# Graph layer, batch norm and attention on one core: a new order for the opening of layer 1 and for the last finished rows

## The chip, the cores and the metric

The kernel runs on one core of a Trainium2 chip. The metric is the device time of one execution in microseconds (us), lower is better; the profile's own clock runs from the first to the last instruction of the core ("the span"). A core has five engines with a queue each, worked off in program order: TensorE (PE, matrix products; its weight loads are PEld), VectorE (DVE), ScalarE (ACT), GpSimd (POOL), and SyncE (SP), which here issues all transfers. Engines wait for each other through semaphores.

## The reference, cut to what matters

Sixteen batches b of 1024 rows with 256 columns pass through two residual layers, each closed by a layer norm over the 256 columns:

```python
# layer 0: graph convolution, two linear maps with batch norm over all batches
x = layernorm(x + bn(relu(bn((A_hat @ x) @ W1.T)) @ W2.T))
# layer 1
c = mean(x, axis=-1)                                   # one number a row
Wg = adj * 2*abs(abs(sigmoid(c[None,:] - c[:,None]) - 0.5) - 0.5)
q  = relu((x.T @ Wg) * para)                           # queries, 4 heads of 64
k, v = split(x @ kv_w)
x = layernorm(x + softmax(q k.T * scale) v)
```

Everything is float32. Because the batch norms of layer 0 average over all batches, layer 1 can't start before the last batch of layer 0 is done.

## The kernel before

Layer 0 ends at about 810 us of the span. It leaves its result transposed in device memory (`yT`). From then on, `fast()` does layer 1 with a queue order that is written out by hand.

**Rows of a batch.** The 1024 rows of a batch are handled as four blocks j of 256 rows. A block goes through: `load` (fetch the transposed y and the residual x; two buffers of each, `LDP = 2`), `bn2_q` (scale and shift on POOL, line L610; for batch 0 `bn2` on ACT, L592), `rows` (DVE transpose L614 and residual add L615; for batch 0 a PE transpose `py`, L626, and an add, L628), `ln1_a` (DVE statistics L558/L559, then POOL makes the scale and shift, L66, L68, L632), `ln1_b` (ACT applies them, L642, and sums each row). For batches 0 and 1, `x1_t` transposes the finished rows on PE (`px`, L671) and DVE copies them to `x1T` (L672). Once the four blocks are there, `means` (DVE, L675 and L677) makes the row means and `crow` lays them along a row by way of a PE transpose `pc` (L688, L692).

**Work that follows the rows.** `gate` / `gate0` makes one of eight 128-row strips of Wg: `wg_a` on ACT (L706, or L708 and L709), `wg_b` on DVE (L715, L716), which takes a strip of adj from a ring of four (`AR = 4`) and asks for the next one. `keys` (`pk`, L732) and `values` (`pv`, L743) are PE products with x1T. `graph` (`pg`, L757; for batch 0 `graph0`, L1076) is the product of the rows and Wg, in eight parts for batch 0, and `queries` (DVE, L765 and L766) makes `qT` from it.

**Attention** runs in 256 steps, 16 a batch. A step has `scores` (PE, L783, into the two PSUM buffers `s`), `exps` (ACT, L795), `sums` (DVE, L801 and L804, the softmax denominators `acc`) and `attend` (PE, L819, into `o`). Four steps make up one half of the rows (hf) with one pair of heads.

**Finished rows.** After each half of a batch: `dens` (PE adds up acc over the partitions, `pd`, L846; ACT copies `dt`, L848), `recips` (PE `pr`, L857; DVE L859), `fetch_o` (the attention output comes back from device memory in another layout, `ob`; in the very last half `back` does this on PE, `pf`, L870), `finish_a` (DVE: transpose L890, product L894, residual L899, statistics; POOL: scale and shift, L66, L68, L903) and `finish_b` (ACT applies them, L911, and the block is stored).

**The order.** `put(w, t, f, ...)` hands piece f to half-turn t of batch w; a batch has NC = 8 half-turns of two steps. The main loop goes in passes of NK = 4 steps (two half-turns): `arrange` sorts all pieces of both half-turns, they are issued first, then the four steps `scores(k+1)`, `exps(k+1)`, `sums(k)`, `attend(k)`. So pieces of a half-turn with odd t are also issued at the start of the pass. The pieces of batch 0 are written out ahead of the loop; `opening(s)` issues gates and `graph0` parts in negative half-turns; and the rows of batch 1 are put there as well, through `put(b - 2, ...)` with b = 1, the four `x1_t` all in the last half-turn before the first attention step.

Of the kernel before, what the change touches and what calls it, by code (L numbers as in the profile page):

```python
# [22 lines left out]
def gnn_norm_attention_kernel(  # L23
# [17 lines left out]
    B, N, C = x.shape  # L41
    H = W1.shape[0]
    NT = N // P
# [3 lines left out]
    NH = N // FB  # L47
# [77 lines left out]
    with ExitStack() as l0:  # L125
# [32 lines left out]
        with ExitStack() as ph1:  # L158
# [9 lines left out]
            for i in range(0, NT, 2):  # L168
                t = hp.tile([P, 2, N], F32, tag="h", name=f"A{i}")
# [29 lines left out]
            for h in range(NH):  # L199
                rows = range(h * KB, (h + 1) * KB)  # L200
# [228 lines left out]
        def load(b, j):  # L429
            shape = [P, CT, 2 * P] if b == 0 else [P, 2, C]  # L430
            yts[b, j] = ldp.tile(shape, F32, tag="yt", name=f"yt{b}_{j}")
            xrs[b, j] = ldp.tile([P, 2, C], F32, tag="xr", name=f"xr{b}_{j}")
            fetch_rows(b, j)
# [16 lines left out]
        with ExitStack() as ph2:  # L450
# [74 lines left out]
            for k, pair in enumerate(pairs):  # L525
# [4 lines left out]
                if not ahead:  # L530
                    for j in range(LDP):
                        load(0, j)
                    for j in range(LDP, NT // 2):
                        t = accp.tile([P, 2, FB], F32, tag="acc", name=f"first{j}")
# [32 lines left out]
    def fast():  # L567
      with ExitStack() as fx:
# [48 lines left out]
        def begin(b):  # L617
            x1Ts[b] = x1Tp.tile([P, CT, N], F32, tag="x1T", name=f"x1T_{b}")
            css[b] = sm.tile([P, NT], F32, tag="cs", bufs=2, name=f"cs_{b}")
# [17 lines left out]
        def ln1_b(b, j):  # L637
            nm, rs = mvs.pop((b, j))
            for a in range(2):
                r = x1s[b, j][:, a, :]  # L640
                i = 2 * j + a
                nc.scalar.activation(  # L642
                    r, r, AF.Identity, bias=nm[:, a : a + 1], scale=rs[:, a : a + 1], accum_out=css[b][:, i : i + 1]
                )
# [22 lines left out]
        def x1_t(b, j):  # L667
            p = ps_t.tile([P, CT, 2 * P], F32, tag="t", name="px")
            for a in range(2):
                for c in range(CT):  # L670
                    nc.tensor.transpose(p[:, c, ts(a, P)], x1s[b, j][:, a, ts(c, P)], ident)  # L671
            nc.vector.tensor_copy(x1Ts[b][:, :, ts(j, 2 * P)], p)  # L672

        def means(b):
            nc.vector.tensor_scalar_mul(css[b], css[b], 1.0 / C)  # L675
            hcs[b] = sm.tile([P, NT], F32, tag="hcs", bufs=2, name=f"hcs_{b}")
            nc.vector.tensor_scalar_mul(hcs[b], css[b], 0.5)  # L677
# [49 lines left out]
        def keys(b, c, h):  # L727
            if h == 0:
                kTs[b, c] = kp.tile([P, N], F32, tag="kT", name=f"kT_{b}_{c}")
            p = ps_t.tile([P, FB], F32, tag="t", name="pk")  # L730
            for k in range(CT):
                nc.tensor.matmul(  # L732
                    p, kvw[:, k, ts(c, P)], x1Ts[b][:, k, ts(h, FB)], start=(k == 0), stop=(k == CT - 1)
                )
            (nc.vector.tensor_copy if b == 0 else nc.scalar.copy)(kTs[b, c][:, ts(h, FB)], p)

        def values(b, j):
            if j == 0:
                vs[b] = vp.tile([P, NT, C], F32, tag="v", name=f"v_{b}")
            p = ps_t.tile([P, FB], F32, tag="t", name="pv")  # L740
            for a in range(2):
                for k in range(CT):
                    nc.tensor.matmul(  # L743
                        p[:, ts(a, C)],
                        x1Ts[b][:, k, ts(j + a, P)],
                        kvw[:, k, C:],
                        start=(k == 0),
                        stop=(k == CT - 1),
                    )
            nc.scalar.copy(vs[b][:, j : j + 2, :], p.rearrange("p (a c) -> p a c", a=2))  # L750
# [57 lines left out]
        def by_pe(b, hf):  # L808
            return b == B - 1 and hf == NH - 1
# [134 lines left out]

        NS = NT // 2 * NP * NH
        NC = NS // 2
        at = {}

        def put(w, t, f, *a):
            at.setdefault(w * NC + t, []).append((f, a))  # L950
# [4 lines left out]
        for b in range(B):  # L955

            for hf in range(NH):
                t = (hf + 1) * (NC // NH)
                put(b, t, dens, b, hf)
                put(b, t, recips, b, hf)  # L960
                for k in range(KB // 2):
                    j = hf * (KB // 2) + k

                    t_a, t_b = (t + 2 + k, t + 6 + k) if hf == 0 else (t + 4 + k, t + 6 + k)
                    if b == B - 1:
                        t_a, t_b = (t + 2 + k, NC + 1) if hf == 0 else (t + 1 + k, t + 2 + k)
                    put(b, t if by_pe(b, hf) else t + 1, back if by_pe(b, hf) else fetch_o, b, j)
                    put(b, t_a, finish_a, b, j)
                    put(b, t_b, finish_b, b, j)
            if b == 0:  # L970
                continue

            put(b - 2, 2, begin, b)
            for j in range(NT // 2):
                put(b - 2, j, load, b, j)
                put(b - 2, j + 1, bn2_q, b, j)
                put(b - 2, j + 2, rows, b, j)
                put(b - 2, j + 2, ln1_a, b, j)
                put(b - 2, j + 3, ln1_b, b, j)
                if b == 1:  # L980
                    put(b - 2, NC - 1, x1_t, b, j)
                    continue
                put(b - 2, j + 3, put_x1, b, j)
                put(b - 2, 5 + j // 2 * 2, get_x1, b, j)
                put(b - 2, min(6 + j, NC), x1_v, b, j)
            put(b - 2, NC - 2, means, b)
            put(b - 2, NC - 1, crow, b)

            i = 0
            for t, n in enumerate(WG):  # L990
                for i in range(i, i + n):
                    put(b - 1, t, gate, b, i)
                i += 1
            kv = [(keys, (b, c, h)) for h in range(NH) for c in range(CT)]
            kv += [(values, (b, j)) for j in range(0, NT, 2)]
            for t, n in enumerate(KV):
                for _ in range(n):
                    f, a = kv.pop(0)
                    put(b - 1, t, f, *a)
            m = 0  # L1000
            for t, n in enumerate(QG):
                for m in range(m, m + n):
                    put(b - 1, NC - len(QG) + t, graph, b, m)
                m += 1
# [66 lines left out]
        def graph0(k):  # L1071
            if k == 0:
                PG0.extend(ps_s.tile([P, 2, FB], F32, tag="s", name=f"pg0_{h}") for h in range(NH))
            for h in range(NH):
                for c in range(CT):
                    nc.tensor.matmul(  # L1076
                        PG0[h][:, c, :],
                        x1s[0, k // 2][:, k % 2, ts(c, P)],
                        wgs[0, k][:, ts(h, FB)],
                        start=(k == 0),  # L1080
                        stop=(k == NT - 1),
                    )
            if k == NT - 1:
                for h in range(NH):
                    for c in range(CT):
                        queries(0, c, h, PG0[h][:, c, :])

        begin(0)
        constants_q()
        for j in range(NT // 2):  # L1090
            bn2(0, j)
        for j in range(NT // 2):
            ln1_a(0, j)
        for j in range(NT // 2):
            ln1_b(0, j)
        x1_t(0, 0)
        x1_t(0, 1)
        keys(0, 0, 0)
        x1_t(0, 2)
        x1_t(0, 3)  # L1100
        means(0)
        crow(0)
        gate0(0)
        keys(0, 1, 0)
        for c in range(CT):
            keys(0, c, 1)
        gate0(1)
        values(0, 0)
        values(0, 2)
        gate0(2)  # L1110
        values(0, 4)
        values(0, 6)

        def opening(s):

            k = s + NC
            if 0 <= k < NC:
                for i in range(3 + 2 * k, min(5 + 2 * k, NT)):
                    gate0(i)
                graph0(k)  # L1120

        NK = NT // 2
        for t in range(min(at) // 2, max(max(at) // 2, nsteps // NK - 1) + 1):
            g = NK * t
            now = [p for s in (2 * t, 2 * t + 1) for p in [(opening, (s,))] + arrange(at.get(s, []))]
            behind = max((k + 1 for k, fa in enumerate(now) if is_short(fa)), default=0)
            for k in range(len(now) + 1):
                if k == behind and 0 <= g < nsteps:  # L1130
                    sums(g)
                if k < len(now):
                    f, a = now[k]
                    f(*a)
            for k in range(g, g + NK):
                if 0 <= k + 1 < nsteps:
                    scores(k + 1)
                    exps(k + 1)
                if 0 <= k < nsteps:
                    if k > g:  # L1140
                        sums(k)
                    attend(k)

        return nc.values_load(
            badi[0][0:1, 0:1],
# [163 lines left out]
```

## Time and profile before

| | |
|---|---|
| time, median of 3 runs | 2493.23 us (2492.45 to 2493.98) |
| span of the profiled run | 2491.2 us, mean granted TensorE clock 0.99 |
| PE busy | 2431.7 us, 98% of the span |
| DVE busy | 1799.9 us, 72% |
| ACT busy | 1097.8 us, 44% |
| POOL busy | 764.1 us, 31% |
| transfers | 288.66 MB, mean 116 GB/s |

PE is busy nearly all the time, so a change can matter in two ways only: through the few places where PE waits, or through the clock that PE is granted. A wait in the trace is read as "engine, tile and line that waited, and the instruction whose end released it".

### The profile page before, as it was taken

The page shows a single profiled execution, that of the slowest core. Times are in us where ns is not written, and L with a number is a line of the kernel's source. Part 1 is how long each engine was busy: PE and PEld are TensorE (multiplying, and loading weights), DVE is VectorE, ACT ScalarE, POOL GpSimd, SP SyncE. Part 2 cuts the span into 40 slices and gives each one's busy share as a digit, 9 for nine tenths or more (in the row PEclk, how much of TensorE's full clock was granted, in tenths as well). Part 3 has the DMA queues.
Part 4 walks back from the last instruction along what each step waited for, and adds up shares of the span by engine and source line. Part 5 has one row for each costly group of instructions (what it writes and reads, how often), then busy time and mean ns, then how long its engine had stood idle before and what let it go on. Part 6 is the DMA issues. An engine that isn't in the chain of part 4 may idle for free. (4 is left out here: it accounts for less than half of the span.)

```text
span 2491.2 us, 33861 instructions
## 1 busy us (share of the span) xinstructions
PE 2431.7 (98%) x12341; PEld 1020.6 (41%) x12341; DVE 1799.9 (72%) x2552; ACT 1097.8 (44%) x1549; POOL 764.1 (31%) x826
## 2 busy tenths in 40 slices
PE   8999999999999889999999999999999999999996
PEld 4444444443444433443434434344344343443432
DVE  5545555555776577888788878888888878888667
ACT  2000000003543455564655646656566465564654
POOL 2222232321656232414324133232341432413002
PEclk9999999999999899999999999999999999999998
DMA  3122222212676443544544535445354454554211
GB/s 135 68 85 102 83 86 85 101 68 84 241 276 235 119 119 76 141 106 116 140 106 119 141 88 144 115 115 148 78 144 106 117 142 97 128 132 98 68 43 41
DMA packets 563118, 288.66 MB, mean 116 GB/s; under 512 B 390664, under 2 KB 535680, under 8 KB 555776
## 3 DMA queue, kind: packets, MB, share of 16 engines
q1 hardware_dynamic: 562944, 286.43, 41.9%
q8 instruction: 99, 1.62, 0.3%
q14 instruction: 75, 0.61, 0.1%
HBM read 192.43 MB, written 93.91 MB: 115 GB/s over the span
## 5 line engine op out<-in xcount | busy, mean ns | idle before, releaser
L795 ACT ACTIVATE e<-s 128x1024 f32<-128x1024 f32 x512 | 496.8, 1022 | 336.9 <-PE s L783 282.0
L804 DVE TENSOR_TENSOR acc<-acc,e 128x1024 f32<-128x1024 f32 x384 | 512.0, 1333 | 117.3 <-ACT e L795 89.7
L783 PE MATMUL s<-qT,kT 64*64 64x512 f32 x4096 | 492.2, 596 | 2.3
L819 PE MATMUL o<-e,v 64*64 64x512 f32 x4096 | 485.3, 589 | 0.0
L757 PE MATMUL pg<-wg,x 128*128 128x512 f32 x960 | 428.9, 597 | 0.0
L610 POOL TENSOR_TENSOR yt<-yt,stq 128x512 f32<-128x512 f32 x120 | 180.1, 1501 | 432.6 <-DMA yt<-yT 353.9
L819 PEld LDWEIGHTS o<-e,v 64*64 64x64 f32 x4096 | 156.6, 133 | 282.8 <-issue 274.3
L757 PEld LDWEIGHTS pg<-wg,x 128*128 128x128 f32 x960 | 177.5, 190 | 231.4 <-issue 227.6
L783 PEld LDWEIGHTS s<-qT,kT 64*64 64x64 f32 x4096 | 147.5, 133 | 295.8 <-issue 261.8
L103 ACT COPY u<-pa 128x512 f32<-128x512 f32 x15 | 8.8, 587 | 475.3 <-PE pa L308 475.3
L716 DVE SCALAR_TENSOR_TENSOR wg<-wg,adj 128x1024 f32<-128x1024 f32 x128 | 162.9, 1303 | 4.0 <-ACT wg L709 1.3
L66 POOL TENSOR_SCALAR rs_z<-mv_z 128x2 f32<-128x2 f32 x64 | 16.8, 262 | 479.7 <-DVE mv_z L559 411.0
L308 PE MATMUL pa<-AhT,x 128*128 128x512 f32 x360 | 161.8, 592 | 0.0
L642 ACT ACTIVATE x<-x,nm_a,rs_a 128x256 f32<-128x256 f32 x128 | 76.3, 598 | 175.5 <-POOL nm_a L632 175.1
L831 DVE TENSOR_TENSOR ot<-o,ot 128x512 f32<-128x512 f32 x64 | 44.3, 692 | 148.0 <-ACT ot L830 148.0
L732 PE MATMUL pk<-x1T,kvw 128*128 128x512 f32 x256 | 122.2, 612 | 1.3 <-DVE x1T L672 1.3
L743 PE MATMUL pv<-kvw,x1T 128*128 128x256 f32 x512 | 117.1, 382 | 0.0
L66 POOL TENSOR_SCALAR rs_a<-mv_a 128x2 f32<-128x2 f32 x64 | 38.8, 606 | 250.4 <-DVE mv_a L559 231.1
L339 PE MATMUL ph<-agg,SW 128*128 128x512 f32 x240 | 112.8, 592 | 0.0
L743 PEld LDWEIGHTS pv<-kvw,x1T 128*128 128x128 f32 x512 | 96.0, 190 | 31.5 <-issue 16.5
L308 PE MATMUL pa<-T,sx 128*128 128x512 f32 x240 | 107.9, 592 | 0.0
L308 PEld LDWEIGHTS pa<-AhT,x 128*128 128x128 f32 x360 | 68.4, 190 | 86.1 <-issue 86.1
(192 smaller groups left out, 3162.8 us busy)
## 6 DMA issues: line engine op xcount, KB each, us to landing
adj<-in_adj_dram SPq DMA_DIRECT2D x128, 512.0 KB, 4.6
h<-hT SPq DMA_DIRECT2D x28, 1024.0 KB, 4.4
hL<-h SPq DMA_DIRECT2D x28, 1024.0 KB, 9.7
x<-in_x_dram SPq DMA_DIRECT2D x16, 1024.0 KB, 7.2
yT<-y SPq DMA_DIRECT2D x64, 256.0 KB, 2.5
out_dram<-r SPq DMA_DIRECT2D x64, 256.0 KB, 2.3
xr<-in_x_dram SPq DMA_DIRECT2D x62, 256.0 KB, 3.7
o<-ot SPq DMA_DIRECT2D x62, 256.0 KB, 2.3
```

The lines of the kernel that those rows point to most:

```text
L308: nc.tensor.matmul(p, xs[n][:, k, :], bs[n][:, k, :], start=(k == 0), stop=(k == KN - 1))
L339: nc.tensor.matmul(p, ws[n][:, ts(f, P)], bs[n], start=True, stop=True)
L610: nc.gpsimd.tensor_tensor(y, y, sc, op)
L642: nc.scalar.activation(r, r, AF.Identity, bias=nm[:, a : a + 1], scale=rs[:, a : a + 1], accum_out=css[b][:, i : i + 1])
L716: nc.vector.scalar_tensor_tensor(t, t, 1.0, adjs[b * NT + i], op0=OP.add, op1=OP.mult)
L732: nc.tensor.matmul(p, kvw[:, k, ts(c, P)], x1Ts[b][:, k, ts(h, FB)], start=(k == 0), stop=(k == CT - 1))
L743: nc.tensor.matmul(p[:, ts(a, C)], x1Ts[b][:, k, ts(j + a, P)], kvw[:, k, C:], start=(k == 0), stop=(k == CT - 1),)
L757: nc.tensor.matmul(pg[b], x1s[b, k // 2][:, k % 2, ts(c, P)], wgs[b, k][:, ts(h, FB)], start=(k == 0), stop=(k == NT - 1))
L783: nc.tensor.matmul(t[r * HD : (r + 1) * HD, h, :], kTs[b, pair][h * HD : (h + 1) * HD, ts(2 * cb + r, HD)], qTs[b, pair, hf][h * HD : (h + ...
L795: nc.scalar.activation(E[g, a], S.pop((g, a)), AF.Exp)
L804: nc.vector.tensor_add(ACC[b, hf, pair], ACC[b, hf, pair], E[g, a])
L819: nc.tensor.matmul(O[b, hf, pair][r][h * HD : (h + 1) * HD, :], vs[b][r * HD : (r + 1) * HD, cb, pair * P + h * HD : pair * P + (h + 1) * HD],
```

## The change

Two things are laid out anew; the arithmetic of every block stays the same, and so does the number of matrix products.

First, the opening of layer 1. The rows of batch 1 are no longer put into negative half-turns. Their first pieces are written out by hand among the pieces of batch 0, and the others follow the parts of `graph0` by a table, one `x1_t` after each of the parts 4 to 7. Within batch 0, the first `x1_t` is ahead of the last `ln1_a`, `values(0, 0)` is ahead of the first `keys`, and `means(0)` ahead of the last two `x1_t`.

Second, the last three halves of the output rows, that is (batch 14, hf 1), (15, 0) and (15, 1). `fetch_o` of the first two is put at half-turn t in place of t + 1, which is the same pass. Their two `finish_a` are put at t (through a new table `between`: issued inside the pass, after two of its four steps) and at t + 2; before, they were at t + 4 and t + 5 for (14, 1), and at t + 2 and t + 3, one pass, for (15, 0). Their `finish_b` are at t + 2 and t + 4 for (14, 1); for (15, 0) one is at t + 2, and only the other stays at NC + 1, the last pieces of all.

```diff
+                    if b * NH + hf < B * NH - 3:
+                        t_f, t_a, t_b = (t + 1, t + 2 + k, t + 6 + k) if hf == 0 else (t + 1, t + 4 + k, t + 6 + k)
+                    elif not by_pe(b, hf):
+                        t_f, t_a, t_b = t, t + 2 * k, t + 2 + 2 * k if b < B - 1 else (t + 2, NC + 1)[k]
+                    else:
+                        t_f, t_a, t_b = t, t + 1 + k, t + 2 + k
+                    put(b, t_f, back if by_pe(b, hf) else fetch_o, b, j)
+                    if t_a == t:
+                        between[(b * NC + t) * 2 + NK // 2] = [(finish_a, (b, j))]
+                    else:
+                        put(b, t_a, finish_a, b, j)
                     put(b, t_b, finish_b, b, j)
...
         begin(0)
         constants_q()
         for j in range(NT // 2):
             bn2(0, j)
-        for j in range(NT // 2):
+        for j in range(NT // 2 - 1):
             ln1_a(0, j)
-        for j in range(NT // 2):
+        ln1_b(0, 0)
+        x1_t(0, 0)
+        ln1_a(0, NT // 2 - 1)
+        load(1, 0)
+        load(1, 1)
+        for j in range(1, NT // 2):
             ln1_b(0, j)
-        x1_t(0, 0)
         x1_t(0, 1)
+        values(0, 0)
         keys(0, 0, 0)
+        means(0)
         x1_t(0, 2)
         x1_t(0, 3)
-        means(0)
+        bn2_q(1, 0)
+        bn2_q(1, 1)
         crow(0)
         gate0(0)
         keys(0, 1, 0)
         for c in range(CT):
             keys(0, c, 1)
         gate0(1)
-        values(0, 0)
+        rows(1, 0)
+        ln1_a(1, 0)
+        load(1, 2)
         values(0, 2)
         gate0(2)
         values(0, 4)
         values(0, 6)
+        rows(1, 1)
+        ln1_a(1, 1)
+        load(1, 3)
+        begin(1)
+        second_rows = {
+            0: [(bn2_q, 2)],
+            1: [(bn2_q, 3)],
+            2: [(ln1_b, 0)],
+            3: [(rows, 2), (ln1_a, 2), (ln1_b, 1)],
+            4: [(x1_t, 0), (rows, 3), (ln1_a, 3)],
+            5: [(ln1_b, 2), (x1_t, 1)],
+            6: [(ln1_b, 3), (x1_t, 2)],
+            7: [(x1_t, 3)],
+        }
...
                 graph0(k)
+                for f, j in second_rows[k]:
+                    f(1, j)
+                if k == NC - 1:
+                    means(1)
+                    crow(1)
...
                     attend(k)
+                for f, a in between.pop(k, ()):
+                    f(*a)
```

More of the change, by code (lines that the diff above doesn't have):

```diff
@@ L946, in fast @@
         NC = NS // 2
-        at = {}
+        NK = NT // 2
+        at, between = {}, {}
         def put(w, t, f, *a):
@@ L962, in fast @@
                     j = hf * (KB // 2) + k
[L964 to L968, printed above, removed]
+                    if b * NH + hf < B * NH - 3:
[9 more added lines that the diff above has]
+                        put(b, t_a, finish_a, b, j)
                     put(b, t_b, finish_b, b, j)
@@ L971, in fast @@
                 continue
-            put(b - 2, 2, begin, b)
-            for j in range(NT // 2):
[L975 to L987, printed above, removed]
+            if b > 1:
+                put(b - 2, 2, begin, b)
+                for j in range(NT // 2):
+                    put(b - 2, j, load, b, j)
+                    put(b - 2, j + 1, bn2_q, b, j)
+                    put(b - 2, j + 2, rows, b, j)
+                    put(b - 2, j + 2, ln1_a, b, j)
+                    put(b - 2, j + 3, ln1_b, b, j)
+                    put(b - 2, j + 3, put_x1, b, j)
+                    put(b - 2, 5 + j // 2 * 2, get_x1, b, j)
+                    put(b - 2, min(6 + j, NC), x1_v, b, j)
+                put(b - 2, NC - 2, means, b)
+                put(b - 2, NC - 1, crow, b)
             i = 0
@@ L1091, in fast @@
             bn2(0, j)
-        for j in range(NT // 2):
+        for j in range(NT // 2 - 1):
             ln1_a(0, j)
-        for j in range(NT // 2):
+        ln1_b(0, 0)
[4 more added lines that the diff above has]
+        for j in range(1, NT // 2):
             ln1_b(0, j)
-        x1_t(0, 0)
         x1_t(0, 1)
+        values(0, 0)
         keys(0, 0, 0)
+        means(0)
         x1_t(0, 2)
         x1_t(0, 3)
-        means(0)
+        bn2_q(1, 0)
+        bn2_q(1, 1)
         crow(0)
@@ L1120, in opening @@
                 graph0(k)
-        NK = NT // 2
-        for t in range(min(at) // 2, max(max(at) // 2, nsteps // NK - 1) + 1):
+                for f, j in second_rows[k]:
[3 more added lines that the diff above has]
+                    crow(1)
+        for t in range(-NC // 2, max(max(at) // 2, nsteps // NK - 1) + 1):
             g = NK * t
```

## The prediction

> **What bounds the kernel now.** I read the page first, then PE's list of waits, then the timelines of all engines around the two places to which those waits led.
>
> ```profile
> PE 2431.7 (98%) x12341; PEld 1020.6 (41%) x12341; DVE 1799.9 (72%) x2552; ACT 1097.8 (44%) x1549; POOL 764.1 (31%) x826
> PE   8999999999999889999999999999999999999996
> PEclk9999999999999899999999999999999999999998
> ```
>
> PE is the bound. It falls below nine tenths only in the first slice, at slices 14 and 15 (810 to 935 us) and in the last. PE's waits, longest first, say for whom:
>
> ```profile
> PE px L671 <- ACT x L642: 6.6, 5, 2.9
> ...
> PE pd L846 <- DVE acc L804: 5.6, 1, 5.6
> PE py L626 <- ACT yt L592: 5.4, 1, 5.4
> PE pc L692 <- DVE x1T L672: 4.6, 1, 4.6
> ```
>
> The change touches px, pc and pd. PE's timeline after batch 0's graph product:
>
> ```profile
> 871.72 0.59 PE L1076 MATMUL pg<-wg,x 128*128 128x512 f32 x1
> 872.15 1.16 PE L671 MATMUL px<-ident,x 128*128 128x128 f32 x8
> 876.26 1.03 PE L671 MATMUL px<-ident,x 128*128 128x128 f32 x4 [2.95 <-ACT x L642]
> 878.81 1.27 PE L671 MATMUL px<-ident,x 128*128 128x128 f32 x4 [1.52 <-ACT x L642]
> 884.64 0.38 PE L692 MATMUL pc<-ident,cs 128*8 128x128 f32 x1 [4.56 <-DVE x1T L672]
> 885.06 1.98 PE L783 MATMUL s<-qT,kT 64*64 64x512 f32 x8
> ```
>
> From 872.3 to 885.1 PE works 3.8 us in 12.8. The rows of batch 1 come late: POOL's bn2_q starts at 857.12, waiting for yT, since `load` was issued at 850.84, behind adj. The end of the program, DVE and PE:
>
> ```profile
> 2458.59 0.71 DVE L890 STREAM_TRANSPOSE r<-ob 128x512 f32<-128x512 f32 x1
> ...
> 2462.02 0.71 DVE L890 STREAM_TRANSPOSE r<-ob 128x512 f32<-128x512 f32 x1
> ...
> 2465.71 7.87 DVE L804 TENSOR_TENSOR acc<-acc,e 128x1024 f32<-128x1024 f32 x6
> ```
> ```profile
> 2467.02 1.05 PE L846 MATMUL pd<-acc,ones 128*32 128x512 f32 x4
> 2473.63 1.92 PE L846 MATMUL pd<-acc,ones 128*32 128x512 f32 x4 [5.57 <-DVE acc L804]
> ```
>
> In the last pass DVE does two finish_a (7.1 us) ahead of six sums (7.9 us), so the sums end 5.6 us after PE is ready for them; and PE then runs at half clock, four pd taking 1.92 in place of 1.05 us.
>
> [...] granted clock 0.50 over 880 to 885 us and over 2473.6 to 2478 us, each behind an idle stretch of 4.6 and 5.6 us. [...] POOL's four instructions of finish_a take 2.7 us at 2443.26, but 5.0 us at 2449.32 beside the L804 sums.
>
> **Opening, front part.** Nothing is added; pieces move. The last py (1.1 us at half clock) now stands behind the first px, so x_0_3's chain ends about 0.9 us later (825.05 for 824.2); nobody on the path waits for it, as px of block 3 comes after pv and pk. `values(0, 0)` needs only block 0 and fills the wait that PE has before pk at 825.49. It starts at about 824.1: eight pv at half clock, 3.5 us, to 827.6. [...] I take full clock from there (before: 0.50 through 825.5 to 830). Then pk x4 at 1.8 (12 took 5.32), px x8 1.2, pc 0.9, to 831.5; means is now ahead of the copies on DVE, so pc's wait of 0.95 us goes; pk x12 5.3 and pv x24 5.3: graph0 starts at 842.1 in place of 844.68, **-2.6 us** (-1 if the half clock lasts as before).
>
> **Opening, rows of batch 1.** Their loads now stand right behind stq in SP's queue (issued to 825.3): 825.3 to about 829. In before, POOL began 6.3 us after the first issue, so I take bn2_q 1,0 at about 832 and, at 2.17 us each, both done by 837. On DVE `rows` and `ln1_a` cost 2.6 us a block (859.33 to 861.97) ahead of gate strips. By DVE's order strip 1 is ready at 839.5, rows 1,0 to 842, strip 2 at 844, rows 1,1 to 846.6, strip 3 at 848.5, strip 4 at 850.5. graph0 needs a strip each 3.45 us (27.63 over 8), so strips 2, 3, 4 at 849, 852.5, 856: DVE stays 4 us and more ahead. Adj strip 7 queues on SP behind load 1,3, which waits for rows 1,1 (847); needed at 866. Blocks 2 and 3 follow at about 856 and 860 on DVE, 2 us each on POOL, 1.1 us on ACT, all before their px. So PE gets through graph0 without a wait. Three of four px (12 at 1.16/8) go between its parts, +1.75 us: graph0 ends at 842.1 + 27.63 + 1.75 = 871.5 (before 872.3).
>
> Then a wait stays. pc stands ahead of the first scores in PE's queue and waits for means; on DVE that stands behind four queries (879.66 to 883.90: 4.24 us), the last x1T copy (0.68) and itself (0.35). With 0.2 us of hand-over: 871.5 + 5.5 = 877.0, pc 0.4, scores at 877.4 in place of 885.06: **-7.7 us** in all, the front part included. PE idles 4.9 us there, so scores begin at half clock as before. From there on PE has no wait to speak of, and the shift should reach the end.
>
> **The last passes.** Three PE stalls are added or changed on the way. (a) Pass of 15, t = 2: ACT has six L911 in place of four ahead of the exps (a pair 1.05 us); PE's scores there already started when the first exp let the s buffer go (2426.76 + 1.02 = 2427.78, scores at 2427.83), so +1.05. POOL's work for the new pair should be done at about 2425, before ACT gets there. (b) Pass t = 4: two L911 stand ahead of dt, for which pr waits: dt 0.6 us later, +0.65. (c) Pass t = 6: two L911 in place of four, but they wait for POOL behind finish_a(15, 0), which runs beside sums: DVE ends 2454, POOL about 2457.1, ACT 2458.2; the exps are then 1 us later than before while PE is 1.7 later, so about -0.25. PE's last attend ends 1.45 us later, at 2468.5. The moved finish_a on DVE (3.4 us each) cost nothing themselves: in before DVE idles 2.9 us ahead of ot in two of these three passes, and more between sums.
>
> The last pass: ot 2457.7, L801 2458.8, one finish_a to 2462.25, six sums of 1.3 us to 2470.1, in place of 2473.6. PE is idle 0.6 us only, so the clock should stay full: pd 1.05, pf 1.16 (2471.1 to 2472.3), pr 0.66, reciprocal at 2473.0 in place of 2478.34: **-5.3 us**. From there to the end the chain is unchanged.
>
> Sum: -7.7 - 5.3 = -13.0, so 2493.2 - 13.0 = **2480.2 us**.
>
> **The rivals.**
> - *Only the opening pays.* POOL is slower beside DVE than I take it (5 us a chain), the L911 wait in (a) and (c) with the exps behind them, and PE loses 2.5 us at each. Then PE itself ends about 5 us later, and what DVE saves at the end is used up: tail 0, 2485.5 us. For it: the 5.0 us chain. Against it: two L911 stand in front in (a), and only two sums run beside.
> - *Only the tail pays.* The loads land late, or DVE falls behind with rows and gates, and graph0 waits as long as was saved: 2487.9. For it: the write of s2/t2 for stq took 8 us to be readable (814.6 to 823.42). Against: I count some 11 us of slack between bn2_q and the time at which strip 2 is needed.
> - *Slower.* Rows 1,0 block DVE's queue, with every later strip behind them, by 11 + 18 us: all strips late, PE cold after it, about 2498 us. Nothing in the profile shows a load of 256 KB that takes so long (xr, of that size, has 3.7 us to landing on the page).
> - *More.* PE stays warm after queries as well (scores x16 at 1.95 in place of 3.61 us), and the stalls (a) to (c) vanish: -17, 2476 us.
>
> **How the numbers follow.** Both pay: 0.64, only the opening 0.14, only the tail 0.10, more 0.08, slower 0.04. The range from 2475.8 to 2487.2 takes in the first two and the last but one, with the front part at -1 and the tail at half; it leaves out the slower case and most of the tail-only case. Faster by over 0.2% (below 2488.2): both, either and more, less a little for the tail-only case that lies on that border: 0.90; same 0.06; slower 0.04.
>
> **What would show it right or wrong.** Right: no wait of px for ACT in the list; graph0 without a gap; one wait of pc on means (DVE L675 or its neighbour) near 5 us; pd waiting under 1 us and pf at full clock. Wrong: a wait of pg for wg on DVE; L614 waiting for POOL near 840; scores in batch 15 waiting for exps by more than 1.5 us a pass.

## The result, and the profile after

The changed kernel takes 2475.22 us (median of 6 runs, 2474.82 to 2478.59); the kernel before, beside it, 2493.61 us (6 runs). The ratio is 0.9929 with a 95% interval of 0.9916 to 0.9941. That is 17.7 us less by the ratio and 18.4 us between the two medians, where 13.0 were forecast. The median lies 0.6 us under the lower end of the forecast range.

The page after, busy times, and the rows of PE and its clock in 40 slices:

```profile
PE 2425.5 (98%) x12341; PEld 1021.1 (41%) x12341; DVE 1806.3 (73%) x2552; ACT 1095.1 (44%) x1549; POOL 767.2 (31%) x826
...
PE   8999999999999899999999999999999999999997
...
PEclk9999999999999899999999999999999999999999
```

The instructions are the same in number. One slice under nine tenths is left at the opening of layer 1 in place of two, and the last slice is fuller. PE's waits, after (what waited, line, for whom, line: us in total, times, longest):

```profile
PE pc L692 <- DVE cs L675: 3.0, 1, 3.0
PE px L671 <- ACT x L642: 2.2, 1, 2.2
...
PE pr L857 <- ACT dt L848: 1.8, 2, 1.1
PE s L783 <- ACT e L795: 1.5, 2, 1.1
...
PE pd L846 <- DVE acc L804: 0.7, 1, 0.7
```

px is down from 6.6 to 2.2 us, pc from 4.6 to 3.0, and waits for another instruction (the means, no longer a PSUM buffer held by an x1T copy); pd is down from 5.6 to 0.7. One line is new, s for e: 1.1 of its 1.5 us are in the pass t = 2 of batch 15, stall (a) of the forecast, and 0.4 at the opening, at 889.4 us. pr is up from 1.4 to 1.8, which is stall (b). PE's timeline from the eighth part of graph0, which stands between the third and the fourth px of batch 1:

```profile
865.44 3.60 PE L1082 MATMUL pg<-wg,x 128*128 128x512 f32 x8
868.88 0.60 PE L671 MATMUL px<-ident,x 128*128 128x128 f32 x4
872.52 0.27 PE L692 MATMUL pc<-ident,cs 128*8 128x128 f32 x1 [3.04 <-DVE cs L675]
872.97 3.45 PE L783 MATMUL s<-qT,kT 64*64 64x512 f32 x16 [0.17 <-issue]
```

The px stand between the parts without a wait. One wait is left, that of pc, and most of the scores behind it run at half clock (the granted clock was 0.60 on average over 872.5 to 876.4 us, and 0.50 over 873.5 to 876.4). The end, DVE and then PE:

```profile
2446.49 0.70 DVE L890 STREAM_TRANSPOSE r<-ob 128x512 f32<-128x512 f32 x1
...
2449.84 7.86 DVE L804 TENSOR_TENSOR acc<-acc,e 128x1024 f32<-128x1024 f32 x6
```
```profile
2456.05 1.05 PE L846 MATMUL pd<-acc,ones 128*32 128x512 f32 x4
2457.76 1.05 PE L846 MATMUL pd<-acc,ones 128*32 128x512 f32 x4 [0.66 <-DVE acc L804]
2458.74 1.09 PE L870 MATMUL pf<-ident,ot 128*128 128x128 f32 x8
2459.67 0.60 PE L857 MATMUL pr<-ident,dt 128*128 128x128 f32 x4
```

One finish_a is left ahead of the last sums, and everything on PE from pd on runs at full clock (1.00 granted over 2456 to 2460.3 us, where the kernel before had 0.50 over 2473.6 to 2478.3): four pd take 1.05 us in place of 1.92.

Layer 0 is the same in all these kernels, yet the first py of layer 1 (the product that waits for ACT's yt, L592) starts between 814.3 and 817.5 us in the profiled runs. Stretches are therefore measured from that first py (815.54 us before, 814.69 after):

| from the first py to | before, us | after, us | moved by |
|---|---|---|---|
| graph0 begins | 29.14 | 25.41 | -3.73 |
| graph0 ends | 56.77 | 54.35 | -2.42 |
| first scores | 69.52 | 58.28 | -11.24 |
| first pd of batch 15's passes (t = 0) | 1592.40 | 1581.30 | -11.10 |
| first pd of the last pass | 1651.48 | 1641.36 | -10.12 |
| last reciprocal (L859) | 1662.80 | 1645.61 | -17.19 |
| end | 1675.66 | 1658.41 | -17.25 |

So in this pair of profiles the opening gave 11.2 us; some 1,500 us of attention carried 11.1 of them through; the last passes first lost 1.0 and then gave 7.1.

### The profile page after: what moved, and what is told of

It reads as the page before. It is cut to its first block, busy times and chain, and to the rows that moved or that the text cites. A ratio compares the mean times of both kernels' runs of the same rounds, so it can differ in the third digit from the quotient of the medians.

```text
span 2473.1 us, 33867 instructions
## 1 busy us (share of the span) xinstructions
PE 2425.5 (98%) x12341; PEld 1021.1 (41%) x12341; DVE 1806.3 (73%) x2552; ACT 1095.1 (44%) x1549; POOL 767.2 (31%) x826
```

## The experiments

Each was timed against the kernel before on the same chip. Times are medians, ratios have their 95% interval.

**The parts one by one.** Four kernels, each with one part of the change only.

The opening alone, the `put` lines of the last passes as in before:

```diff
-                    if b * NH + hf < B * NH - 3:
...
+                    t_a, t_b = (t + 2 + k, t + 6 + k) if hf == 0 else (t + 4 + k, t + 6 + k)
+                    if b == B - 1:
+                        t_a, t_b = (t + 2 + k, NC + 1) if hf == 0 else (t + 1 + k, t + 2 + k)
...
```

> Only the opening is changed; the last passes are as before. Theory (the two parts are independent and PE-bound work lies between them): the first scores come 11 to 12 us earlier, and all of it reaches the end: about -11.5 us, 2482 us. Rival (the parts share the gain; most of the 18 us is the tail's, since an earlier opening is absorbed by the batches in between): -5 us or less, 2488 us.

Measured: 2482.33 us, ratio 0.9957 (0.9941 to 0.9974), -10.4 us between the medians. The theory holds: the attention here, which PE bounds, hands the earlier start through to the end. In the trace the scores start 58.02 us from the first py, 11.5 us earlier than before.

The last passes alone, the opening as in before:

> Only the last passes are changed; the opening is as before. Theory: the reciprocal of the last half comes 6.1 us earlier measured from the last attend-bound stretch, so -6 us, 2487 us, with pd waiting under 1 us and the pf and pr transposes at full clock. Rival (the tail gains nothing by itself, because the extra ACT work ahead of the exps takes it back): within 2 us of before.

Measured: 2486.82 us, ratio 0.9976 (0.9966 to 0.9987), -5.9 us. As expected, pd waits 0.7 us, and pf and pr take 1.09 and 0.60 us. The two halves add up within their intervals: 10.4 + 5.9 = 16.3 us between medians, for 18.4 of the whole. From the first py to the end the traces give 12.0 and 6.4 us, for 17.25 of the whole.

The order inside batch 0 alone (the edit of the opening without every line that names batch 1):

```diff
...
+        ln1_b(0, 0)
         x1_t(0, 0)
+        ln1_a(0, NT // 2 - 1)
...
         x1_t(0, 1)
+        values(0, 0)
         keys(0, 0, 0)
+        means(0)
...
```

> Only the order inside batch 0 is changed (first px ahead of the last py, values(0,0) ahead of keys, means ahead of the last px); the rows of batch 1 stay in the negative half-turns, the last passes are as before. Theory A (each edit pays by itself): graph0 starts 3.7 us earlier and the scores too: -3.7 us, 2490 us. Theory B (the late rows of batch 1 set the first scores as soon as graph0 ends earlier): graph0 starts 3.7 us earlier, but px waits for ACT by so much longer, since the loads of these rows stand behind adj strips and hardly move: 0 to -1.5 us.

Measured: 2489.41 us, ratio 0.9988 (0.9980 to 0.9997), -3.3 us between medians. From the first py, graph0 begins at 25.51 us and the first scores at 66.32, earlier by 3.6 and 3.2 us. PE's timeline of batch 0 shows where they come from. In the kernel before:

```profile
825.49 3.78 PE L732 MATMUL pk<-x1T,kvw 128*128 128x512 f32 x4 [1.31 <-DVE x1T L672]
...
831.73 1.06 PE L688 MATMUL pc<-ident,cs 128*128 128x128 f32 x8 [0.95 <-DVE cs L675]
```

In this kernel:

```profile
823.48 3.15 PE L743 MATMUL pv<-kvw,x1T 128*128 128x256 f32 x8
826.47 1.88 PE L732 MATMUL pk<-x1T,kvw 128*128 128x512 f32 x4
...
829.30 1.06 PE L688 MATMUL pc<-ident,cs 128*128 128x128 f32 x8
```

Values fill the wait of pk, the wait of the first pc is gone, and four pk take 1.88 us in place of 3.78 (the same four take 1.88 in the changed kernel, at a granted clock of 1.00 over 826 to 828 us, and 3.78 in the kernel before, at 0.50 over 825.5 to 830). Theory A holds. Theory B had overlooked that the loads of batch 1 move too: they stand behind adj strips, which are asked for by gates, and the gates came earlier as well. The first load is issued 31.65 us from the first py, 3.65 earlier than before.

The rows of batch 1 alone, batch 0's own order as before:

```diff
...
         means(0)
+        bn2_q(1, 0)
+        bn2_q(1, 1)
         crow(0)
...
         gate0(1)
+        rows(1, 0)
+        ln1_a(1, 0)
+        load(1, 2)
         values(0, 0)
...
```

> Only the rows of batch 1 are moved among the gate strips and the parts of graph0; batch 0's own order and the last passes are as before. Theory A: graph0 starts as before, ends 1.3 us later for three px in it, and the wait after it shrinks from 12.8 to about 4 us: -7.5 us, 2486 us. If theory B of the run with batch 0's order alone is right, the two runs add up to less than the whole opening (11 to 12 us).

Measured: 2485.36 us, ratio 0.9969 (0.9957 to 0.9982), -7.4 us. From the first py the scores start at 61.69 us, 7.8 earlier. 3.2 and 7.8 make 11.0 of the 11.2 us of both: the two parts add up too.

**Why the opening gave 3.5 us more than forecast.** I had put all four queries behind the end of graph0. The DVE timeline after has the first one before it:

```profile
867.36 0.69 DVE L765 TENSOR_TENSOR qT<-pg,para_sb 128x512 f32<-128x512 f32 x1 [1.03 <-PE pg L1082]
...
872.21 0.16 DVE L675 TENSOR_SCALAR cs<-cs 128x8 f32<-128x8 f32 x1
```

graph0 works to 869.04 us, but the two queries of h = 0 read a tile that is finished halfway through the last part. To test it, the last part takes h = 1 first:

```diff
-            for h in range(NH):
+            for h in range(NH) if k < NT - 1 else (1, 0):
                 for c in range(CT):
                     nc.tensor.matmul(
                         PG0[h][:, c, :],
```

> The changed kernel with one swap: in the eighth part of graph0 the half h = 1 is multiplied ahead of h = 0, while the queries keep their order (h = 0 first). Theory (my working put all four queries behind the end of graph0, but those of h = 0 start when the first half of the last part is done, 1.7 us earlier): the first query starts 1.7 us later, and pc and the scores with it: +1.5 us against the changed kernel, wait of pc near 4.7 us. Rival (the earlier scores come from elsewhere, a faster DVE or a shorter px): the wait of pc stays at 3.0 us and the time within 0.5 us.

In its timelines the first query starts behind the end of the product, and pc waits by so much longer; first DVE, then PE:

```profile
870.37 0.69 DVE L765 TENSOR_TENSOR qT<-pg,para_sb 128x512 f32<-128x512 f32 x1 [2.75 <-PE pg L1082]
```
```profile
875.53 0.37 PE L692 MATMUL pc<-ident,cs 128*8 128x128 f32 x1 [4.76 <-DVE cs L675]
876.00 3.69 PE L783 MATMUL s<-qT,kT 64*64 64x512 f32 x16
```

The wait is 4.76 in place of 3.04 us, 1.7 longer, as the theory said; scores start 59.75 us from the first py, 1.5 later. The keys behind them take 7.84 us in place of 7.28. The time, 2478.69 us with a ratio of 0.9944 (0.9927 to 0.9960), has the same sign, 3.5 us above the changed kernel's median where 1.5 were expected; the two intervals overlap, so that the size rests on the trace.

**What is left of that wait.** pc waits for means, and means stands on DVE behind queries that it doesn't need. ln1_b(1,3) is done at 863.7 us, well before. So:

```diff
...
+                if k == NC - 1:
+                    crow(1)
                 graph0(k)
+                if k == NC - 2:
+                    ln1_b(1, 3)
+                    means(1)
                 for f, j in second_rows[k]:
                     f(1, j)
-                if k == NC - 1:
-                    means(1)
-                    crow(1)
```

> The changed kernel with ln1_b(1,3) and means(1) behind the seventh part of graph0 and crow(1) ahead of the eighth, so that pc and the means are done before the queries. Theory (pc's wait is only DVE's order, and the scores need only the queries): no wait of pc; the first scores start when the queries of h = 0 are done (about 2.2 us after the first of them) and the second tile when all four are; PE idle after graph0 about 2 us in all[...]: 16 scores in about 2 us of work in place of 3.45; -3 to -4 us against the changed kernel, 2471.5 us. Rival (keys and gates of batch 1 or the s buffers bind next): -1 us or less.

Its PE timeline behind graph0 and the last px:

```profile
868.88 1.09 PE L783 MATMUL s<-qT,kT 64*64 64x512 f32 x8
870.76 1.09 PE L783 MATMUL s<-qT,kT 64*64 64x512 f32 x8 [0.79 <-DVE qT L765]
871.78 1.55 PE L732 MATMUL pk<-x1T,kvw 128*128 128x512 f32 x3
```

The wait of pc is gone, what is left is 0.79 us for the last query, and the granted clock is 1.00 over 868 to 876 us. keys (pk) begin 57.44 us from the first py, 4.2 earlier than in the changed kernel. 2470.44 us, ratio 0.9910 (0.9893 to 0.9927): by the ratios 4.7 us better than the changed kernel's 0.9929. The intervals of the two overlap a little, but its four times (2469.91 to 2470.51 us) lie below every time of the changed kernel (2474.10 to 2478.59). The theory holds.

**The tail: wait or clock?** The change shortens DVE's work ahead of the last sums, and PE also keeps its clock (1.00 granted in place of 0.50, as above). To take the second alone, the kernel before got products of no use in the gap between the two halves of pd:

```diff
                     nc.tensor.matmul(p[k : k + 32, :], ones32, acc[:, h, :], start=True, stop=True)
+                if by_pe(b, hf) and pair == 0:
+                    z = ps_t.tile([P, FB], F32, tag="t", name="pz")
+                    for _ in range(FILL):
+                        nc.tensor.matmul(z[:32, :], ones32, acc[:, 0, :], start=True, stop=True)
```

With FILL = 12:

> The kernel before, with 12 products of no use on PE in the last pass between the two halves of pd, to keep PE busy while it waits for DVE. Theory (some 2 us of the tail's gain is the clock that PE keeps, not the wait): granted clock stays at 1.0, pd x4 1.05 in place of 1.92, pf and pr about 1.1 and 0.6 in place of 1.97 and 1.06; -1.8 us against before. Rival (clock irrelevant, since DVE and ACT pace the end): within 0.5 us of before.

Measured: 2494.73 us, ratio 1.0008 (0.9999 to 1.0017): no gain, where 1.8 us were expected. The products behind the filling did take what they take in the changed kernel at a granted clock of 1.00 (pf 1.09 us, pr 0.60), but the filling took 9.2 us in a gap of 5.6, so the second half of pd came 3 us late. This run therefore can't tell what the clock is worth. Six products end inside the gap, so FILL = 6:

> The kernel before with 6 in place of 12 products of no use between the two halves of pd: each takes 0.85 us (two records of 0.43), so 12 ran 2.9 us past the point at which DVE was done, and 6 should end by then. Theory (some 2 us of the tail's gain is the clock that PE keeps): from the first pd to the reciprocal 9.3 us in place of 11.3; -2 us against before. Rival: no change, within 0.5 us of before.

```profile
2465.71 1.05 PE L847 MATMUL pd<-acc,ones 128*32 128x512 f32 x4
2466.59 5.31 PE L851 MATMUL pz<-acc,ones 128*32 128x512 f32 x12
2472.33 1.05 PE L847 MATMUL pd<-acc,ones 128*32 128x512 f32 x4 [0.42 <-DVE acc L805]
2473.31 1.09 PE L875 MATMUL pf<-ident,ot 128*128 128x128 f32 x8
2474.24 0.60 PE L862 MATMUL pr<-ident,dt 128*128 128x128 f32 x4
```

In this kernel's PE timeline pd, pf and pr have the lengths that they have in the changed kernel, though DVE's order is that of before. From the first pd to the reciprocal it takes 9.17 us (2465.71 to 2474.88) in place of 11.32: 2.15 us for the clock (1.00 granted over 2466 to 2474 us), since the second half of pd starts 6.6 us behind the first in both. The time is 2490.47 us, ratio 0.9992 (0.9985 to 0.9999), -2.05 us between medians. The changed kernel has 4.25 us there (2456.05 to 2460.30). Its pd waits 0.66 us in place of 5.57, 4.9 less; with the 2.15 of the clock that makes up its gain of 7.1 us.

**Does moving (15, hf 0) alone suffice?** What stood ahead of the last sums was (15, hf 0). A kernel that moves it alone and finishes (14, hf 1) as before:

```diff
-                    if b * NH + hf < B * NH - 3:
+                    if b < B - 1:
```

> The changed kernel, but (14, hf 1) finished where it was before (finish_a at t + 4 and t + 5, finish_b at t + 6 and t + 7), so that of the last passes only (15, hf 0) is moved. Theory (DVE's work is a queue: the pass t = 4 of batch 15 then holds three finish_a of 3.4 us beside its sums, some 20 us of DVE work in a 16 us pass, and hands the excess to the last pass): pd waits for acc nearly as long as before, 4 to 5.5 us, and PE's clock falls again; 5 us slower than the changed kernel, 2480 us. Rival (the gain comes from (15, hf 0) alone, as it was what stood ahead of the last sums): as the changed kernel, 2475 us.

Measured: 2482.44 us, ratio 0.9960 (0.9944 to 0.9975), against 2476.34 for the changed kernel beside it on the same chip: 6.1 us lost, about all that the tail had given. The size was near what the theory said, the way was not. pd doesn't wait at all. ACT's and PE's timelines show where the time is:

```profile
2450.16 2.07 ACT L911 ACTIVATE r<-r,nm,rs_z 128x256 f32<-128x256 f32 x4 [5.69 <-POOL nm L903]
```
```profile
2453.20 3.69 PE L783 MATMUL s<-qT,kT 64*64 64x512 f32 x16 [6.90 <-ACT e L795]
```

DVE is late with the third finish_a of the pass (it starts at 2442.40 us, where the changed kernel starts it at 2438.25), so POOL is (done at 2450.4 for 2445.3), so finish_b on ACT waits 5.7 us at the start of the last pass, and the exps stand behind it: PE loses 6.9 us, and its clock (0.66 on average over 2448 to 2456 us; 3.69 us for 16 scores). That is the way of the forecast's first rival, "the L911 wait ... with the exps behind them", for which it took 2.5 us in each of two passes; here one pass loses 6.9. In the changed kernel the same instruction waits 0.4 us:

```profile
2445.09 1.09 ACT L911 ACTIVATE r<-r,nm,rs_z 128x256 f32<-128x256 f32 x2 [0.37 <-POOL nm L903]
```

So finishing (14, hf 1) earlier is needed as well, to keep the third finish_a out of that pass.

**The stalls that the change added.** In the changed kernel's ACT timeline six L911 stand ahead of the exps:

```profile
2412.82 3.06 ACT L911 ACTIVATE r<-r,nm,rs_z 128x256 f32<-128x256 f32 x6
2415.78 1.91 ACT L795 ACTIVATE e<-s 128x1024 f32<-128x1024 f32 x2
```

A kernel that issues the five finish_b of these passes between steps:

```diff
...
-                    put(b, t_b, finish_b, b, j)
+                    g0 = {(B - 2, 0): 4, (B - 2, 1): 5, (B - 2, 2): 6, (B - 2, 3): 8, (B - 1, 0): 12}.get((b, j))
+                    if g0 is None:
+                        put(b, t_b, finish_b, b, j)
+                    else:
+                        between.setdefault((B - 1) * NS + g0, []).append((finish_b, (b, j)))
```

> The changed kernel with the five finish_b of the last passes issued between steps (one behind each exps) in place of the start of a pass. Theory (the extra PE waits of the last passes, 1.1 us for exps and 0.4 us for dt, are ACT work standing ahead of exps and dt, and ACT idles 1.4 us a step): the two waits go, -1.5 us against the changed kernel, 2473.7 us. Rival (DVE's sums bind at the end instead, so that an earlier PE just waits for pd): pd's wait grows from 0.66 to over 1.5 us and the time stays within 0.5 us.

In its ACT timeline each pair lies in ACT's idle time behind the exps, as here:

```profile
2415.33 1.08 ACT L911 ACTIVATE r<-r,nm,rs_z 128x256 f32<-128x256 f32 x2
```

Of the wait of s for e, the 1.1 us in these passes are gone; 0.3 us at the opening are left. pr waits 1.4 us in place of 1.8, pd still waits 0.7, and from the first py to the first pd of the last pass it takes 1639.55 us, 1.8 less than in the changed kernel. The time can't tell it by itself: 2475.16 us, four runs from 2472.49 to 2477.52, ratio 0.9931 (0.9914 to 0.9947).

**Both refinements together,** beside the changed kernel once more:

> The changed kernel once more, beside the two that are built on it, so that they can be set against it on one chip: about 2475 us.

> The changed kernel with both refinements: means(1) and crow(1) ahead of the last part of graph0, and the five finish_b of the last passes between steps. Theory (the two lie in stretches that share nothing but PE): the sum of the two, about -4.4 and -1.7 us against the changed kernel, 2469 us. Rival (only the first shows in the time): 2470.5 us.

2476.34 us (ratio 0.9933, 0.9919 to 0.9946) and 2469.03 us (ratio 0.9905, 0.9889 to 0.9920). The second has the lowest time of all kernels run here, 23.5 us under before. That is 7.3 us between medians, somewhat more than the 4.2 and 1.8 us that the traces show for the two; the sum was expected, and the rival's 2470.5 us lies above all four times (2468.39 to 2469.47).

## Why the prediction was right where it was, and where it was not

*Bound and mechanism: right.* PE bounds the kernel, the two places were the ones named, the parts do what was said, and nearly nothing between them absorbs the shift (11.24 us at the first scores, 11.10 a whole layer later). In the second profile of the changed kernel, taken with its repeated timing, the two are 11.09 and 10.15: there s waits 1.19 us for e at the opening, in place of 0.42. So the gain of the opening is known to about 1 us; the stretch from the first pd of batch 15's passes to the last reciprocal is the same in both profiles within 0.02 us.

*Front part of the opening, -2.6: right in kind, -3.73 measured.* values(0, 0) fills the wait as described, and pc no longer waits for means. Full clock from 827.6 us was my estimate; it came back sooner: the granted clock was 0.50 over 821 to 825.5 us and 1.00 over 825.5 to 830, so that keys, px and pc together took 3.7 us (826.03 to 829.76) in place of the 3.9 forecast, behind a shorter values (2.9 from its start to that of keys, for 3.5).

*Rows of batch 1 among gates: right.* rows 1,0 was forecast to end by 842 on DVE and ended at 840.9; no gate strip kept PE waiting. Of the signs that the forecast named, "no wait of px for ACT" is not met as it is worded: 2.2 us are left, all of them at the first px of batch 0 (820.3 us), where 2.2 of the 6.6 us before were as well. The px of batch 1 wait no more. Three px cost 0.43 us each, 1.3 in all, in place of 1.75: I had priced them as in a group of eight, with its last end.

*The wait of pc behind the queries: the mis-sized term.* From the end of graph0 to the scores I forecast 5.9 us; it is 3.93. The step that failed is that means "stands behind four queries", all of them counted from the end of graph0; half of them run beside its last 1.7 us, as the swapped kernel showed. The forecast gained 1.1 us too little in the front part, 0.4 at the px and 2.0 at the queries; these are the 3.5 us that were missing.

*The stalls, +1.45 in all: +0.98 measured.* (a) 1.0 of 1.05, (b) 0.4 of 0.65, (c) -0.4 of -0.25, by PE's starts before and after. The finish_a that goes through `between` comes behind the third of the four steps of its pass, not the second as told above: DVE starts it at 2438.25 us, behind the sums of three steps.

*The last pass, -5.3 with the stalls in it: -6.1 measured.* Half a microsecond is from the stalls, the rest from a shorter chain of pd, pf and pr. That the clock would stay was right (1.00 over 2456 to 2460.3 us, behind a wait of 0.66), and is worth 2 of it.

*The clock: forecast rightly, but one reading was wrong.* That the scores behind pc would begin at half clock came true for all but the first half microsecond (0.77 granted over 873 to 873.5 us, 0.50 over 873.5 to 876.4), though PE's wait was 3.0 us and not the 4.9 forecast. The 0.50 over 880 to 885 us in the kernel before does not stand behind the wait of 4.6 us, which began at 880.1: the granted clock was 1.00 over 877.5 to 878 us, 0.73 over the next half microsecond and 0.50 from there. It fell behind a wait of 2.95 us and 0.9 us of px, in the wait of 1.52 us that came next, and the px at 878.81 us, 1.27 us for four, ran at half clock already.

*The rivals.* "Only the opening pays" didn't happen here, but its mechanism is real: it appears when (15, hf 0) is moved alone. "Only the tail pays" and "slower" didn't happen: PE's list after has no wait of pg for wg. "More" at 2476 us came closest in time, by another way than I gave it: PE didn't stay warm after the queries (0.60, as above), and the stalls were there. The range was too narrow at that end, since I had taken the later of two bounds for the queries without looking at which tile each one reads.

## What to carry to other kernels

Where one engine bounds a kernel and works through it almost without a gap, as here (98% busy), an opening or an end that is shortened by x us was worth about x us (11.24 us at the first scores, 11.10 a layer later), and parts that lie in different gaps added up (3.2 and 7.8 us to 11.0 of 11.2); look for the instruction in each gap that the waiting one doesn't need, such as queries ahead of means here (4.7 us). Count a consumer from the end of the tile that it reads, not from the end of the group of products that the tile belongs to (1.7 us here). Finishing work on an engine that is idle on the average (ACT, 44% busy) stood ahead of what the bound engine waits for when it was issued at the start of a pass (six L911 in place of four, 3.06 us, ahead of the exps: PE waited 1.1 us): put it behind the instruction that feeds the bound engine, and spread it so that no pass holds more than that engine can do in it.

## What the runs showed of the hardware that I had not expected

Six products of no use, 5.3 us of PE time in a gap in which PE had to wait anyway, made the kernel before 2 us faster: the 16 PE instructions behind the gap took 2.5 us in place of 4.7, at a granted clock of 1.00 (over 2466 to 2474 us) in place of 0.50 (over 2473.6 to 2478.3 us in the kernel before). The interval of that gain is 0.2 to 3.7 us; the trace gives 2.15. In the changed kernel PE stood still for 3.0 us ahead of one pc of 0.27 us, and the 16 scores behind it took 3.45 us (0.60 granted over 872.5 to 876.4 us), where those of the kernel with means first, with a gap of 0.79 us between them, took 2.2 us of PE time (1.00 over 868 to 876 us). In the kernel before, the clock fell at about 878.2 us (1.00 over 877.5 to 878, 0.50 over 878.5 to 885); in the 4.9 us ahead of that PE had worked for 0.9 us and had had no wait longer than 2.95.
